# A two-layer graph network: the multiply by the adjacency matrix, split between VectorE and GpSimd two heads to two or one head to three

## The chip, the cores and the metric

One core of a Trainium2 chip runs the whole program. The metric is the device time in microseconds (us). A core has a matrix engine (TensorE, PE in the profile), a vector engine (VectorE, DVE), an activation engine (ScalarE, ACT), a general engine (GpSimd, POOL), a queue engine for transfers (SyncE, SP), an on-chip memory (SBUF) of 128 partitions, and an accumulator memory for TensorE's results (PSUM). Each engine runs its own instructions in order; engines wait for each other by semaphores.

## The reference

Two layers over the same 4096 x 4096 weighted adjacency matrix `adj`, with 4096 nodes of 512 features. Layer 0 is attention with `adj` added to its scores. Layer 1, where the change is, is a graph attention with 8 heads of 64 features:

```python
x = x + _L0_gnn_ref(h, adj, adj, Wq, bq, Wk, bk, Wv, bv)
h = jnp.maximum(_layernorm(x, axis=-1), 0.0)
...
nX = (x @ W).reshape(n, NHEAD, OUT_DIM).transpose(1, 0, 2)
nX = a_ln * (nX - mean) / (std + EPS) + b_ln
at1 = jnp.einsum('kno,ok->kn', nX, a1)[:, :, None]
at2 = jnp.einsum('kno,ok->kn', nX, a2)[:, :, None]
kg = at1 + at2.transpose(0, 2, 1)
kg = jax.nn.leaky_relu(kg, negative_slope=LK_ALPHA)
kg = kg * graph[None, :, :]
mg = jnp.where(mask[None, :, :], kg, NEG_FILL)
attention = jax.nn.softmax(mg, axis=-1)
y = attention @ nX + nX
return jax.nn.elu(y)
```

`graph` and `mask` are both `adj`. For each pair of nodes and each head the kernel must form a leaky logit, multiply it by the pair's weight, take the exponent and sum the features of the neighbours.

## The kernel before

**Layer 0** makes q, k and v, walks over 32 blocks of 128 rows, and on the way writes a transposed copy of `adj` to memory (`gT_d`, scaled by 0.2, and `nT_d`, a large negative number where a pair is not connected). Nothing of it is touched.

**Layer 1's start** (lines 316 to 453) projects the features, normalizes them per head into `nX`, and computes the two numbers per node and head that the logits are made of. It isn't touched either, but it runs GpSimd and VectorE instructions of width 512 whose lengths are of use: L405 and L399 on GpSimd, L396 and L397 on VectorE.

**Layer 1's loop** (lines 455 to 673) has 512 steps: 8 blocks of 512 target nodes (`ic`), 2 groups of 4 heads (`hg`), 32 blocks of 128 source nodes (`jt`). The 32 steps of one `(ic, hg)` are called a group in what follows; there are 16. The logits of a step lie transposed, source nodes on the partitions, in a tile `t` of 128 x 4 heads x 512 float32; five such tiles rotate. A step `n` consists of:

- `z_sums` (L513, L518): TensorE adds both numbers and the negative mask into PSUM, in two halves of two heads (tile `d`, three buffers).
- `relu` (L525): ScalarE makes the positive part for heads 0 and 1.
- `leaky` (L533 twice, L537): VectorE makes the logits, two heads by a maximum and an addition of PSUM (L533, 512 wide each), two by an addition of PSUM (L537, 1024 wide).
- `weigh` (L543 to L545): the multiply by the adjacency block `g`.
- `exponent` (L548): ScalarE takes the exponent of all four heads.
- `values` (L561): TensorE sums the features of the source nodes, eight matmuls.

The loop is software-pipelined by hand: iteration `n` issues `values(n-3)`, `exponent(n-2)`, `weigh(n-1)`, `leaky(n)`, `z_sums(n+1)`, `relu(n+1)`, in this order. Every engine follows this source order, since `seq` is `tc.keep_in_program_order`. So on VectorE the multiply of one step stands in front of the logits of the next one.

Three steps after a group's last one, `finish` starts its closing work, spread over the next iterations: a copy of the sums (L570 on ScalarE, L571 on VectorE); `rows_of` in the two iterations after, where TensorE turns the sums (L582) and VectorE divides them (L589 copy, L591 reciprocal, L592 a minimum over `low` and `tot`, L594 twice, all this for two halves); then `own` twice (L602, a GpSimd addition of width 512); `exps` on ScalarE (L609 to L611); `close` twice (L615 on VectorE, L619 on GpSimd, both of width 512), and a store. These stand after `leaky` and before the next `weigh` in each engine's order.

`weigh` before, with `gate` a tile of one column that nothing else reads:

```python
g = loads[n // JB][0][:, STEPS[n][2] % JB, :].unsqueeze(1).to_broadcast([P, 2, GC])
t = logits[n]
seq(nc.vector.tensor_mul(t[:, 0:2, :], t[:, 0:2, :], g))
seq(nc.gpsimd.tensor_mul(gate, t[:, 0, 0:1], t[:, 0, 0:1]))
seq(nc.gpsimd.tensor_mul(t[:, 2:4, :], t[:, 2:4, :], g))
```

The gate instruction (L544) reads a column that VectorE's multiply (L543) writes. GpSimd, which runs in order, therefore starts its own multiply (L545) only after VectorE's. The blocks of `g` come by transfers of four steps at a time (L466), two rounds ahead, into three buffers.

Of the kernel before, what the change touches and what calls it, by code (L numbers as in the profile page):

```python
# [10 lines left out]
F32 = mybir.dt.float32  # L11
# [7 lines left out]
P = 128  # L19
# [16 lines left out]
GC = 512  # L36
# [9 lines left out]
@with_exitstack  # L46
def adj_preln_gnn_kernel(
    ctx: ExitStack,
    tc: tile.TileContext,
    x: bass.AP,  # L50
    adj: bass.AP,
    wqT: bass.AP,
    bq: bass.AP,
    wkT: bass.AP,
    bk: bass.AP,
    wvT: bass.AP,
    bv: bass.AP,
    w1: bass.AP,
    a1T: bass.AP,
    a2T: bass.AP,  # L60
    a_ln: bass.AP,
    b_ln: bass.AP,
    out: bass.AP,
):
    nc = tc.nc
    keep = ctx.enter_context(tc.tile_pool(name="keep", bufs=1))
    flag = keep.tile([1, 1], mybir.dt.int32, name="flag")
    fast_path(
        tc, flag, x, adj, wqT, bq, wkT, bk, wvT, bv, w1, a1T, a2T, a_ln, b_ln, out
    )  # L70

    low = nc.values_load(flag[0:1, 0:1])
    with tc.If(low > 0):
        general_path(tc, x, adj, wqT, bq, wkT, bk, wvT, bv, w1, a1T, a2T, a_ln, b_ln, out)
# [3 lines left out]
def fast_path(  # L78
# [18 lines left out]
    nc = tc.nc  # L97
# [51 lines left out]
    with tc.tile_pool(name="kv", bufs=1) as kv:  # L149
# [3 lines left out]
        with tc.tile_pool(name="proj_c", bufs=1) as pc, tc.tile_pool(  # L153
            name="proj", bufs=2
# [45 lines left out]
        with tc.tile_pool(name="attn", bufs=2) as work, tc.tile_pool(  # L200
            name="attn_ps", bufs=2, space=PSUM
# [95 lines left out]
    gat = ctx.enter_context(tc.tile_pool(name="gat", bufs=1))  # L297
# [10 lines left out]
    HB = HD + 1  # L308
    back = gat.tile([P, 2, HB], F32, name="back")
    fours = gat.tile([P, P], BF16, name="fours")  # L310
    gate = gat.tile([P, 1], F32, name="gate")

    with tc.tile_pool(name="gat_c", bufs=1) as pc, tc.tile_pool(name="gat_w", bufs=2) as work, tc.tile_pool(
        name="gat_ps", bufs=2, space=PSUM
# [140 lines left out]
    with tc.tile_pool(name="ga", bufs=2) as work, tc.tile_pool(name="ga_ps", bufs=2, space=PSUM) as psum:  # L455
        JB = 4
        seq = tc.keep_in_program_order
        STEPS = [(ic, hg, jt) for ic in range(NI) for hg in range(NH // HG) for jt in range(NB)]
        n_steps = len(STEPS)
        loads, logits, zs, groups = {}, {}, {}, {}  # L460
# [77 lines left out]

        def weigh(n):

            g = loads[n // JB][0][:, STEPS[n][2] % JB, :].unsqueeze(1).to_broadcast([P, 2, GC])
            t = logits[n]
            seq(nc.vector.tensor_mul(t[:, 0:2, :], t[:, 0:2, :], g))  # L543
            seq(nc.gpsimd.tensor_mul(gate, t[:, 0, 0:1], t[:, 0, 0:1]))  # L544
            seq(nc.gpsimd.tensor_mul(t[:, 2:4, :], t[:, 2:4, :], g))  # L545

        def exponent(n):
            seq(nc.scalar.activation(logits[n], logits[n], AF.Exp, bias=shift))  # L548
# [93 lines left out]
        for n in range(n_steps + 14):  # L642
            if n % JB == 0 and n // JB + 2 < n_steps // JB:
                load_adj(n // JB + 2)
            if n < n_steps and STEPS[n][2] == 12:
                load_rows(n)
            if 0 <= n - 3 < n_steps:
                values(n - 3)
                if n % JB == 2:
                    loads.pop((n - 3) // JB)  # L650
            if 0 <= n - 2 < n_steps:
                exponent(n - 2)
            if 0 <= n - 1 < n_steps:
                weigh(n - 1)
            if n < n_steps:
                leaky(n)
            if n + 1 < n_steps:
                if STEPS[n + 1][2] == 0:
                    open_group(n + 1)
                z_sums(n + 1)  # L660
                relu(n + 1)
            if 0 <= n - 3 < n_steps and STEPS[n - 3][2] == NB - 1:
                finish(n, *STEPS[n - 3][:2])
            for f in later.pop(n, []):
                f()
# [411 lines left out]
```

## Time and profile before

| What | Value |
|---|---|
| Median of 3 runs | 4892.43 us (4891.4 to 4892.91) |
| The profiled execution's own time | 4892.91 us |
| Its span in the profile | 4891.1 us |
| Busy share of the span: PE, DVE, ACT, POOL | 90%, 63%, 42%, 32% |
| First and last start of L545 (layer 1's loop) | 2751.3 and 4867.8 us |
| DVE busy in 3500 to 4000 us | 478.23 of 500 us |
| PE busy in 3500 to 4000 us | 438.97 of 500 us |
| ACT and POOL busy in 3500 to 4000 us | 366.72 and 335.11 us |

The span is the time from the first to the last instruction that the profiler saw; the execution's own time lies 1.8 us above it. The shares over the whole span mix layer 0, in which TensorE is busiest, with layer 1's loop; the lower rows show the loop alone. POOL's busy time includes time in which an instruction of it has started and stands. Lines are named as in the profile, L543 for line 543; after the change the same code has numbers that are one lower up to the multiply on VectorE, and two lower behind it.

### The profile page before, as it was taken

To read this page: it belongs to the slowest core of one execution; us is meant where nothing else is said; L and a number is where in the kernel's file an instruction comes from. 1 tells how busy PE (TensorE), PEld (TensorE's weight loads), DVE (VectorE), ACT (ScalarE), POOL (GpSimd) and SP (SyncE) were. 2 spreads that over 40 slices of the span, in tenths; PEclk is the share of its full clock that TensorE was granted. 3 is DMA by queue.
4 is the path that set the end of the run, shared out by engine and by line. 5 is a ranking of instruction groups with operands and counts; after the bars stand their busy time and mean duration, and the time that the engine had idled before them with its cause. 6 is when DMAs were issued, how large, how long until landed. Compare 5 with 4: busy or idle time off the path is not lost.

```text
span 4891.1 us, 46208 instructions
## 1 busy us (share of the span) xinstructions
PE 4392.4 (90%) x16036; PEld 1780.2 (36%) x16036; DVE 3067.9 (63%) x5059; ACT 2057.5 (42%) x1908; POOL 1544.6 (32%) x1222
## 2 busy tenths in 40 slices
PE   8999999999999999999745588888888888888887
PEld 3444444444444444444322122222222222222222
DVE  3215333333333333333377799999999999999998
ACT  1112222112121211211111477777777777777776
POOL 0000000000000000000133466666766666666666
PEclk9999999999999999999867799999999999999999
DMA  2115333333233333332211333333333333333332
GB/s 88 48 30 164 96 98 98 97 92 94 91 94 97 97 97 98 97 98 75 66 56 55 115 120 114 115 108 121 123 112 120 114 116 113 115 118 114 110 113 74
DMA packets 521508, 484.23 MB, mean 99 GB/s; under 512 B 168624, under 2 KB 424624, under 8 KB 517168
## 3 DMA queue, kind: packets, MB, share of 16 engines
q1 hardware_dynamic: 229632, 371.24, 23.3%
q10 hardware_dynamic: 291632, 109.95, 8.0%
q8 instruction: 128, 2.10, 0.2%
q14 instruction: 116, 0.95, 0.1%
HBM read 342.69 MB, written 138.41 MB: 98 GB/s over the span
## 4 chain that ended last, share of the span: by engine, by line
PE 54%; DVE 30%; issue 12%; POOL 3%; DMA 1%; ACT 1%; SPq 0%; ACTq 0%; POOLq 0%; DVEq 0%
PE acc L257 18%; PE ps L238 18%; DVE t L533 13%; DVE t L537 10%; PE acc L561 3%; PE pq L175 2%; PE pv L195 2%; PE pk L186 2%; PE pg L220 2%; DVE t L543 2%; PE d L518 2%; PE pt L265 2%; POOL prod L405 2%; POOL own L399 1%; PE d L513 1%
## 5 line engine op out<-in xcount | busy, mean ns | idle before, releaser
L545 POOL TENSOR_TENSOR t<-t,g 128x1024 f32<-128x1024 f32 x512 | 1213.8, 2371 | 1.7 <-issue 1.6
L561 PE MATMUL acc<-t,nX 128*64 128x512 f32 x4096 | 1016.0, 618 | 47.5 <-ACT ob L570 24.7
L548 ACT ACTIVATE t<-t,shift 128x2048 f32<-128x2048 f32 x512 | 1019.6, 1991 | 2.4 <-POOL t L545 2.4
L257 PE MATMUL acc<-v,pT 128*128 128x512 f32 x2048 | 924.2, 594 | 2.6 <-ACT pT L267 0.4
L238 PE MATMUL ps<-kT,qt 128*128 128x512 f32 x2048 | 887.6, 593 | 0.7 <-DVE m L241 0.7
L401 POOL MEMSET nX<- 128x8 f32 x32 | 3.6, 113 | 2576.0 <-DVE full L396 2576.0
L525 ACT ACTIVATE t<-d 128x1024 f32<-128x1024 f32 x512 | 524.7, 1025 | 560.3 <-PE d L518 560.3
L533 DVE SCALAR_TENSOR_TENSOR t<-u,at2m,d 128x512 f32<-128x512 f32 x1024 | 713.3, 735 | 21.2 <-PE d L518 21.2
L543 DVE TENSOR_TENSOR t<-t,g 128x1024 f32<-128x1024 f32 x512 | 684.6, 1337 | 15.1
L267 ACT COPY pT<-pt 128x512 f32<-128x512 f32 x256 | 146.8, 586 | 1284.1 <-PE pt L265 1249.7
L537 DVE TENSOR_TENSOR t<-t,d 128x1024 f32<-128x1024 f32 x512 | 618.3, 1208 | 1.7 <-ACT t L525 1.2
L513 PE MATMUL d<-z,z 6*128 6x512 bf16 x2048 | 375.1, 386 | 204.5 <-DVE t L533 192.5
L238 PEld LDWEIGHTS ps<-kT,qt 128*128 128x128 f32 x2048 | 386.0, 190 | 470.6 <-issue 461.2
L518 PE MATMUL d<-nb,ident_b 128*128 128x512 bf16 x2048 | 547.4, 391 | 0.0
L257 PEld LDWEIGHTS acc<-v,pT 128*128 128x128 f32 x2048 | 369.2, 190 | 378.5 <-issue 368.2
L222 DVE TENSOR_SCALAR ng<-pg 128x512 bf16<-128x512 f32 x256 | 176.7, 691 | 459.2 <-PE pg L220 405.3
L561 PEld LDWEIGHTS acc<-t,nX 128*64 128x64 f32 x4096 | 253.2, 139 | 568.7 <-issue 464.4
L241 DVE CUSTOM_DVE_ANT_0 s<-ps,s 128x512 f32<-128x512 f32 x256 | 174.0, 690 | 449.8 <-PE ps L238 449.6
L513 PEld LDWEIGHTS <-z 6*128 6x128 bf16 x2048 | 92.4, 91 | 748.8 <-issue 703.4
L544 POOL TENSOR_TENSOR gate<-t 128x1 f32<-128x1 f32 x512 | 99.4, 194 | 707.6 <-DVE t L543 659.2
L224 ACT ACTIVATE gs<-pg 128x512 f32<-128x512 f32 x256 | 153.6, 600 | 328.0 <-DVE ng L222 243.4
L225 DVE SCALAR_TENSOR_TENSOR gs<-ng,gs 128x512 f32<-128x512 bf16 x256 | 174.0, 690 | 160.7 <-ACT gs L224 160.5
(118 smaller groups left out, 2886.4 us busy)
## 6 DMA issues: line engine op xcount, KB each, us to landing
g<-gT_d SPq DMA_DIRECT2D x128, 1024.0 KB, 5.4
s<-in_adj_dram SPq DMA_DIRECT2D x32, 2048.0 KB, 8.3
gT_d<-gs ACTq DMA_DIRECT2D x256, 256.0 KB, 2.3
nb<-nT_d SPq DMA_DIRECT2D x128, 512.0 KB, 3.6
nT_d<-ng ACTq DMA_DIRECT2D x256, 128.0 KB, 2.0
z<-z_d SPq DMA_DIRECT2D x144, 128.0 KB, 2.1
xt<-in_x_dram SPq DMA_DIRECT2D x8, 1024.0 KB, 5.3
q_d<-qs SPq DMA_DIRECT2D x32, 256.0 KB, 3.1
```

The source lines that it names most:

```text
L222: nc.vector.tensor_scalar(ng, pt, 0.0, NEG_BIG, ALU.is_equal, ALU.mult)
L238: nc.tensor.matmul(ps, qt[:, k, :], kT[:, k, ts(c, 512)], start=k == 0, stop=k == KC - 1)
L257: nc.tensor.matmul(acc, pT[:, ts(t, P)], v[:, j, :], start=j == 0, stop=j == NB - 1)
L513: seq(nc.tensor.matmul(pair[hh // 2][:, hh % 2, :], z2[rows, ts(jt % JB, P)], groups[ic, hg]["z1"][rows, :], start=True, stop=False,))
L518: seq(nc.tensor.matmul(pair[hh // 2][:, hh % 2, :], ident_b, ng[:, jt % JB, :], start=False, stop=True))
L525: seq(nc.scalar.activation(t[:, 0:2, :], zs[n][0], AF.Relu, scale=4.0))
L533: seq(nc.vector.scalar_tensor_tensor(t[:, 2 + e, :], u4[:, e, :], at2m[:, jt, h : h + 1], pair[1][:, e, :], ALU.max, ALU.add,))
L537: seq(nc.vector.tensor_add(t[:, 0:2, :], t[:, 0:2, :], pair[0]))
L543: seq(nc.vector.tensor_mul(t[:, 0:2, :], t[:, 0:2, :], g))
L545: seq(nc.gpsimd.tensor_mul(t[:, 2:4, :], t[:, 2:4, :], g))
L548: seq(nc.scalar.activation(logits[n], logits[n], AF.Exp, bias=shift))
L561: seq(nc.tensor.matmul(grp["acc"][hf][ts(e, HD), :], nX[:, jt, hg * HG + 2 * hf + e, :], t[:, 2 * hf + e, :], start=jt == 0, stop=jt == NB ...
```

## The change

In `weigh` the multiply by `g` is cut differently. VectorE takes one head (512 elements per partition) in place of two, GpSimd three (1536) in place of two. The gate instruction and its tile go, so nothing orders the two multiplies of a step any more: both wait for what wrote their part of `t`, which on both is VectorE's L537 of the same step. The order on each engine, given by `seq`, stays, and so do the results.

```diff
-    gate = gat.tile([P, 1], F32, name="gate")
...
         def weigh(n):
 
-            g = loads[n // JB][0][:, STEPS[n][2] % JB, :].unsqueeze(1).to_broadcast([P, 2, GC])
+            g = loads[n // JB][0][:, STEPS[n][2] % JB, :]
             t = logits[n]
-            seq(nc.vector.tensor_mul(t[:, 0:2, :], t[:, 0:2, :], g))
-            seq(nc.gpsimd.tensor_mul(gate, t[:, 0, 0:1], t[:, 0, 0:1]))
-            seq(nc.gpsimd.tensor_mul(t[:, 2:4, :], t[:, 2:4, :], g))
+            seq(nc.vector.tensor_mul(t[:, 0, :], t[:, 0, :], g))
+            seq(nc.gpsimd.tensor_mul(t[:, 1:4, :], t[:, 1:4, :], g.unsqueeze(1).to_broadcast([P, 3, GC])))
```

## The prediction

> **What bounds the kernel now.** I read the page's table of costly groups first, then the timeline of layer 1's loop for each engine alone, then the stretches where VectorE and GpSimd overlap. The groups give the price of each instruction (engine, operation, shapes, count, busy us, mean ns, idle time before):
>
> ```profile
> L545 POOL TENSOR_TENSOR t<-t,g 128x1024 f32<-128x1024 f32 x512 | 1213.8, 2371 | 1.7 <-issue 1.6
> ...
> L533 DVE SCALAR_TENSOR_TENSOR t<-u,at2m,d 128x512 f32<-128x512 f32 x1024 | 713.3, 735 | 21.2 <-PE d L518 21.2
> L543 DVE TENSOR_TENSOR t<-t,g 128x1024 f32<-128x1024 f32 x512 | 684.6, 1337 | 15.1
> ```
>
> The loop runs 512 steps, and in most of them VectorE's timeline (start, length, both in us) is this:
>
> ```profile
> 3734.36 1.39 DVE L533 SCALAR_TENSOR_TENSOR t<-u,at2m,d 128x512 f32<-128x512 f32 x2
> 3735.68 1.21 DVE L537 TENSOR_TENSOR t<-t,d 128x1024 f32<-128x1024 f32 x1
> 3736.92 1.26 DVE L543 TENSOR_TENSOR t<-t,g 128x1024 f32<-128x1024 f32 x1
> 3738.10 1.39 DVE L533 SCALAR_TENSOR_TENSOR t<-u,at2m,d 128x512 f32<-128x512 f32 x2
> ```
>
> Each starts when the one before ends, and the step is 3738.10 - 3734.36 = 3.74 us. So VectorE is the bound. GpSimd is not:
>
> ```profile
> 3734.58 0.19 POOL L544 TENSOR_TENSOR gate<-t 128x1 f32<-128x1 f32 x1 [1.22 <-DVE t L543]
> 3734.72 2.38 POOL L545 TENSOR_TENSOR t<-t,g 128x1024 f32<-128x1024 f32 x1
> ```
>
> It idles 1.22 us a step until L543 is done, since the gate instruction L544 reads what L543 wrote. The two multiplies by g therefore never run side by side in this step. TensorE is close behind: in the stretch 3734.36 to 3738.10 it is busy 3.54 of 3.74 us. ScalarE has 2.91.
>
> Where a stray GpSimd instruction breaks that order, the trace shows what running side by side costs:
>
> ```profile
> 3697.01 2.37 POOL L545 TENSOR_TENSOR t<-t,g 128x1024 f32<-128x1024 f32 x1
> ...
> 3698.25 2.21 DVE L543 TENSOR_TENSOR t<-t,g 128x1024 f32<-128x1024 f32 x1
> ...
> 3699.34 2.26 POOL L602 TENSOR_TENSOR y<-y,own 128x512 f32<-128x512 f32 x1
> ...
> 3701.55 0.19 POOL L544 TENSOR_TENSOR gate<-t 128x1 f32<-128x1 f32 x1
> ```
>
> L543 needs 1.21 us alone and took 2.21: it stood until L545 was through, and then ran. L602 needs 1.26 us alone (the last two have that) and took 2.26: it stood until L543 was through. They alternate and do not share, and VectorE, waiting since 3698.25, went ahead of the GpSimd instruction queued behind L545. This is so in every group of the loop. Even a tiny operand is caught, in the tail:
>
> ```profile
> 4877.90 1.26 POOL L602 TENSOR_TENSOR y<-y,own 128x512 f32<-128x512 f32 x1 [7.74 <-DVE tot L589]
> 4877.92 0.18 DVE L591 RECIPROCAL rinv<-tot 128x4 f32<-128x4 f32 x1
> 4878.02 1.16 DVE L592 TENSOR_TENSOR low<-low,tot 128x4 f32<-128x4 f32 x1
> ```
>
> L592 is usually 0.13 us; here it stood about 1.03 us for L602. L533 and L537 keep their lengths beside L545.
>
> **What the Trainium skill says.** "SBUF — State Buffer", section "Who interferes with whom": a VectorE instruction with two SBUF inputs contends with a GpSimd instruction that reads SBUF, the one that starts second blocks fully; one with at most one SBUF input does not contend. The trace agrees on both: L543 and L592 have two SBUF inputs, L533 and L537 take their pair from PSUM. The page doesn't say who goes first when both wait; the trace above does. "GPSIMD Engine Reference", section 3.1, has GpSimd 1.96 times slower at a two-input operation; here 2.371 against 1.21 us, the same ratio.
>
> **The change, part by part.**
> (1) VectorE's multiply shrinks from 1024 to 512 elements. The same shape in the projection (L396) takes 0.67 us, so VectorE's own work per step falls by 0.53 us to about 3.2.
> (2) GpSimd's grows to 1536. 128x512 takes 1.265 (L405) and 128x1024 2.371, so 1.106 per further 512: 3.477 us. Instructions queued back to back overlap by about 0.04, so 3.44 from start to start.
> (3) The gate goes: 512 times 0.19 us of GpSimd, which lay in idle time, and with it the order. GpSimd now waits for L537 of its step, as VectorE's multiply does. VectorE starts it at once; GpSimd comes second, and stands.
> (4) What VectorE's multiply adds to GpSimd's cycle. In the stretch above, L602 and the 1024-wide L543 together took 3701.55 - 3699.34 = 2.21 from GpSimd's start to its next start; L602 alone is 1.265 - 0.04. The insertion costs 0.985 for 1024 elements, less 0.535 for the 512 that go: 0.45 us. Ends: 0.67 if nothing of it overlaps; as low as 0.3 if more does.
>
> The steady step: 3.44 + 0.45 = 3.89 us, against 3.745 (the usual distance of L545's starts): +0.15. VectorE has its 2.5 us of L533 and L537 done before GpSimd releases, so its next multiply always waits there first and the alternation is stable. ScalarE's exponent waits for GpSimd later by a microsecond in each step, with several tiles t in hand (five buffers), and TensorE has 0.35 us a step to spare: both stay hidden. The loads of g are two rounds ahead and stay so.
>
> (5) The ends of the 15 groups before the last; there seven steps are unusual. I call L537's end zero.
> - The two steps with the row sums (L589 to L594) last 7.6 us each on average. VectorE there waits 1.9 us for TensorE's L582 (1.3 in the second), and GpSimd stands behind the gate. Without the gate it runs in this hole, and L592 runs into it. First step: GpSimd is still at the step before until +0.75, then at this step's multiply until +4.2; L592, due at +2.2, stands until then; 1.32 us of the rest, 0.62 of multiply and 2.52 of L533 and L537 follow: 8.6 us. Second: GpSimd runs from +0.1 to +3.5, L592 stands from +1.55, and its second copy at +4.3 meets L602, which has just started (as in the tail): about 1.03 more, 9.0 in all. So +1.0 and +1.4.
> - The two steps with L602 take 4.68 each now. The first L602 has gone into the step before: 3.9, so -0.8. The second: 3.44 + 0.45 + 1.22 = 5.1, so +0.4.
> - The two with L615 and L619 take 5.3 now. L615 has two SBUF inputs and stands for GpSimd; then its 0.65, the multiply 0.55, L619 1.15 and 3.4 of GpSimd follow one another: 5.8, so +0.5 twice.
> - The step with L571's copy has 4.18 now and hides it: -0.3.
> Sum per group +2.7 us. From below it is 0, where TensorE's delays cover the lock; from above 5.
>
> Sum: 512 - 15 x 7 = 407 steps x 0.15 = 61, and 15 x 2.7 = 40: +101 us. The tail changes by well under 1. The profiled execution has span 4891.1, ran 4892.91, and the median is 4892.43. 4891.1 + 101 is 4992 for the span and 4994 for the median. Nothing is left to hide it: no other engine waits long enough elsewhere.
>
> **The rivals.**
> A, faster. VectorE's short multiply slips past GpSimd's long one for less than 0.30 us, the 3.745 - 3.44 from which this decides. With none at all, TensorE's 3.54 becomes the bound: 407 x 0.2 = 83, and some 1.5 us at each group's end, 22: about 4787. For it: VectorE is the bound and loses 0.53 us a step. Against it: 1024 elements cost 0.985, and even 4 elements stood 1.03 us.
> B, much slower. When GpSimd releases, its own queued multiply goes first, and VectorE waits for two. Then two steps take 0.55 + 3.44 + 3.44 + 0.55 + 2.6 = 10.6 us, 5.3 each: 407 x 1.55 = 631, with the ends about 5565. For it: both wait at that moment. Against it: L543 won that meeting in each group's end.
> C, no change: the step comes out between 3.73 and 3.76, and the ends even out: 4892. It asks for an insertion of 0.3 exactly.
> That the change doesn't do what it says is out: GpSimd's instruction stream shows one 128x1536 multiply a step, no gate, waiting for VectorE's addition.
>
> **The numbers.** Forecast 0.85, A 0.06, B 0.06, C 0.03. The forecast's own ends: with 3.40 for the 1536 multiply and no cost at the groups' ends the step is 3.81 and the sum +27, 4920; with 0.67 of insertion and 5 us at the ends it is 407 x 0.37 + 75 = 226, 5118. Few of these ends meet, so I take 4935 to 5085. A change of 0.2% (10 us) is what a measurement of this kernel can tell from none. Faster 0.06, same 0.03, slower 0.91.
>
> **What would show it.** Right: L545's successor near 3.45 to 3.5 us with GpSimd busy nearly without a gap in the steady steps; VectorE's multiply stretched from 0.67 to about 1.3 by its wait; step 3.89; L592 at up to 2 us, 30 or more times. Wrong: if VectorE's multiply stays at 0.67 beside GpSimd's (A), or if it lasts 4 us in every second step (B). If GpSimd's 1536 elements take more than 3.6 us, (2) is mis-sized.

## The result and the profile after

The median is 4962.89 us (4961.42 to 4965.52, 4 runs) against 4891.91 before in the same comparison; the ratio is 1.0147, with a 95% interval of 1.0129 to 1.0164. The change makes the kernel 71 us slower. The span of the profiled execution went from 4891.1 to 4959.5, +68.4 us.

Some groups of the page after the change (L543 is now GpSimd's multiply, L542 VectorE's, L532 and L536 what were L533 and L537):

```profile
L543 POOL TENSOR_TENSOR t<-t,g 128x1536 f32<-128x1536 f32 x512 | 1950.4, 3843 | 147.7 <-DVE t L536 76.4
...
L532 DVE SCALAR_TENSOR_TENSOR t<-u,at2m,d 128x512 f32<-128x512 f32 x1024 | 713.4, 735 | 26.9 <-DMA g<-gT_d 16.3
...
L542 DVE TENSOR_TENSOR t<-t,g 128x512 f32<-128x512 f32 x512 | 668.6, 1306 | 15.1
```

VectorE's multiply has half the elements and still 1306 ns on average (1337 before): the saving has gone into standing. L532 keeps its 735 ns. GpSimd has 147.7 us of idle time left before its multiplies. Before the change it idled 707.6 us before its gates, most of it for VectorE's multiply:

```profile
L544 POOL TENSOR_TENSOR gate<-t 128x1 f32<-128x1 f32 x512 | 99.4, 194 | 707.6 <-DVE t L543 659.2
```

VectorE's timeline in the steady part, and GpSimd's row from the same stretch (three multiplies merged into one row of 11.65 us):

```profile
3658.63 1.40 DVE L542 TENSOR_TENSOR t<-t,g 128x512 f32<-128x512 f32 x1
3659.43 11.65 POOL L543 TENSOR_TENSOR t<-t,g 128x1536 f32<-128x1536 f32 x3
3659.95 1.39 DVE L532 SCALAR_TENSOR_TENSOR t<-u,at2m,d 128x512 f32<-128x512 f32 x2
3661.26 1.21 DVE L536 TENSOR_TENSOR t<-t,d 128x1024 f32<-128x1024 f32 x1
3662.50 1.38 DVE L542 TENSOR_TENSOR t<-t,g 128x512 f32<-128x512 f32 x1
```

The step is 3662.50 - 3658.63 = 3.87 us. VectorE looks as full as before, but of L542's 1.39 us about 0.7 is waiting (it takes 0.67 alone). A row's length is the time from start to end, with the standing in it: a busy engine need not be the one that works.

The two steps with the row sums in one group, first VectorE's timeline, then GpSimd's, same stretch:

```profile
3712.05 1.31 DVE L590 TENSOR_TENSOR low<-low,tot 128x4 f32<-128x4 f32 x1
...
3719.15 2.06 DVE L590 TENSOR_TENSOR low<-low,tot 128x4 f32<-128x4 f32 x1
...
3721.81 1.16 DVE L590 TENSOR_TENSOR low<-low,tot 128x4 f32<-128x4 f32 x1
```

```profile
3709.87 3.47 POOL L543 TENSOR_TENSOR t<-t,g 128x1536 f32<-128x1536 f32 x1
3717.74 3.46 POOL L543 TENSOR_TENSOR t<-t,g 128x1536 f32<-128x1536 f32 x1 [4.40 <-issue]
3721.69 1.26 POOL L600 TENSOR_TENSOR y<-y,own 128x512 f32<-128x512 f32 x1 [0.50 <-DVE tot L587]
```

Four elements per partition take up to 2.06 us. Each of the three ends within 0.1 us of GpSimd's instruction (3713.34, 3721.20, 3722.95): L590 stands for it. Of all 64, 33 took over 1 us. Their minimum, median and maximum (in ns) follow; before, the median was 131:

```profile
L590 DVE TENSOR_TENSOR low<-low,tot x64: 129/1124/2069, 2885.6 to 4946.4; 128x4 f32<-128x4 f32 x64
```

Where the 68.4 us lie, from the starts of L537 (L536 after) in all 512 steps, as means over the 15 groups after the first:

| Steps of a group | Before, us | After, us | Difference |
|---|---|---|---|
| two with the row sums | 7.59 + 7.57 | 8.61 + 8.81 | +2.26 |
| the one after them | 3.75 | 3.39 | -0.36 |
| two with GpSimd's first additions | 4.75 + 4.62 | 4.22 + 4.53 | -0.61 |
| the one with L571's copy | 4.18 | 3.87 | -0.31 |
| three with the last additions | 14.32 | 15.21 | +0.89 |
| the other 23 | 86.5 | 89.1 | +2.6 |

That is +4.5 a group. The 15 groups give 67 us and the first group 2.8; the loop began 2.6 earlier, and what follows its last step took 0.8 longer.

### The profile page after: what moved, and what is told of

The parts are those of the page before. It is cut to its first block, busy times and chain, and to the rows that moved or that the text cites. A ratio compares the mean times of both kernels' runs of the same rounds, so it can differ in the third digit from the quotient of the medians.

```text
span 4959.5 us, 44909 instructions
## 1 busy us (share of the span) xinstructions
PE 4410.4 (89%) x16036; PEld 1779.5 (36%) x16036; DVE 3118.6 (63%) x5059; ACT 2059.9 (42%) x1908; POOL 2168.7 (44%) x710
## 4 chain that ended last, share of the span: by engine, by line
PE 47%; DVE 26%; issue 12%; POOL 4%; ACT 2%; DMA 1%; ACTq 0%; SPq 0%; DVEq 0%; POOLq 0%
PE acc L257 18%; PE ps L238 17%; DVE t L532 11%; DVE t L536 9%; PE acc L559 3%; PE d L517 3%; PE pg L220 2%; PE pt L265 2%; POOL t L543 2%; POOL prod L404 2%; DVE t L542 1%; DVE low L590 1%; PE d L512 1%; POOL own L398 1%; PE pt L580 1%
## 5 line engine op out<-in xcount | busy, mean ns | idle before, releaser
L543 POOL TENSOR_TENSOR t<-t,g 128x1536 f32<-128x1536 f32 x512 | 1950.4, 3843 | 147.7 <-DVE t L536 76.4
L559 PE MATMUL acc<-t,nX 128*64 128x512 f32 x4096 | 1046.8, 634 | 56.9 <-ACT t L546 32.2
L532 DVE SCALAR_TENSOR_TENSOR t<-u,at2m,d 128x512 f32<-128x512 f32 x1024 | 713.4, 735 | 26.9 <-DMA g<-gT_d 16.3
L542 DVE TENSOR_TENSOR t<-t,g 128x512 f32<-128x512 f32 x512 | 668.6, 1306 | 15.1
L536 DVE TENSOR_TENSOR t<-t,d 128x1024 f32<-128x1024 f32 x512 | 618.5, 1208 | 6.9 <-ACT t L524 5.3
L512 PE MATMUL d<-z,z 6*128 6x512 bf16 x2048 | 357.9, 388 | 245.3 <-DVE t L532 196.9
L517 PEld LDWEIGHTS <-ident_b 128*128 128x128 bf16 x2048 | 161.0, 99 | 249.0 <-issue 133.4
```

The source lines that it names most:

```text
L512: seq(nc.tensor.matmul(pair[hh // 2][:, hh % 2, :], z2[rows, ts(jt % JB, P)], groups[ic, hg]["z1"][rows, :], start=True, stop=False,))
L517: seq(nc.tensor.matmul(pair[hh // 2][:, hh % 2, :], ident_b, ng[:, jt % JB, :], start=False, stop=True))
L532: seq(nc.vector.scalar_tensor_tensor(t[:, 2 + e, :], u4[:, e, :], at2m[:, jt, h : h + 1], pair[1][:, e, :], ALU.max, ALU.add,))
L536: seq(nc.vector.tensor_add(t[:, 0:2, :], t[:, 0:2, :], pair[0]))
L542: seq(nc.vector.tensor_mul(t[:, 0, :], t[:, 0, :], g))
L543: seq(nc.gpsimd.tensor_mul(t[:, 1:4, :], t[:, 1:4, :], g.unsqueeze(1).to_broadcast([P, 3, GC])))
```

## The experiments

Two theories stood for the steady step. L: the two multiplies exclude each other, and VectorE's is inserted into each cycle of GpSimd's. G: GpSimd's 1536 elements simply take that long.

**No multiply on VectorE.** One head of each four is left unweighted.

```diff
-            seq(nc.vector.tensor_mul(t[:, 0, :], t[:, 0, :], g))
             seq(nc.gpsimd.tensor_mul(t[:, 1:4, :], t[:, 1:4, :], g.unsqueeze(1).to_broadcast([P, 3, GC])))
```

> The changed kernel without VectorE's multiply: head 0 of each group of four isn't multiplied by g, the rest is as after the change. Theory L (the two multiplies exclude each other, and VectorE's adds 0.42 us to each cycle of GpSimd's): the steady step falls from 3.87 to what is next, GpSimd's 3.44 or TensorE's 3.54, and the time from 4963 to about 4800 to 4820. Theory G (no exclusion, GpSimd's 1536 elements simply need 3.87 us): the step stays at 3.87 and the time within 20 us of 4950.

Measured: 4738.36 us, ratio 0.9681 (0.9665 to 0.9697). The steady step is 3.42 to 3.43 us, with GpSimd busy without a gap. GpSimd's group:

```profile
L542 POOL TENSOR_TENSOR t<-t,g 128x1536 f32<-128x1536 f32 x512 | 1754.9, 3472 | 131.5 <-issue 57.0 <-DVE t L536 46.1 <-DMA xi<-x_d 25.3
```

The same instruction that has a mean of 3843 ns beside VectorE's multiply has 3472 without it. G is out. The insertion of 512 elements costs 3.87 - 3.425 = 0.445 us. The time came out 62 us below the lower end of what L had expected, since I had taken TensorE's busy 3.54 us as a floor; TensorE kept up with 3.42. In a stretch of the first group (2766.3 to 2782.1 us), while GpSimd, at 3.43 us a multiply, was falling behind, the steps even took 3.16 us, with TensorE busy 15.75 of 15.80 us.

**The new split, with the gate kept.**

```diff
-            seq(nc.vector.tensor_mul(t[:, 0:2, :], t[:, 0:2, :], g))
+            seq(nc.vector.tensor_mul(t[:, 0, :], t[:, 0, :], g))
             seq(nc.gpsimd.tensor_mul(gate, t[:, 0, 0:1], t[:, 0, 0:1]))
-            seq(nc.gpsimd.tensor_mul(t[:, 2:4, :], t[:, 2:4, :], g))
+            seq(nc.gpsimd.tensor_mul(t[:, 1:4, :], t[:, 1:4, :], g.unsqueeze(1).to_broadcast([P, 3, GC])))
```

> The kernel before with the new split, one head to three, but with the gate kept. Theory L: GpSimd's release, then VectorE's multiply 0.55, the semaphore and the gate 0.29, then 3.43 of GpSimd, one after the other: a steady step of 4.27 and a time of about 5105; L592 stays at 0.13 us and the two steps with the row sums go back to about 7 us. Theory G: VectorE's multiply has long been done when GpSimd comes to the gate, which adds 0.15 only: 4.0 us a step, 4990.

Measured: 5127.97 us, ratio 1.0478 (1.046 to 1.0495); the steady step is 4.29, the row-sum steps 7.09 and 7.0 on average. Both engines, from VectorE's timeline and from GpSimd's:

```profile
3826.66 1.21 DVE L537 TENSOR_TENSOR t<-t,d 128x1024 f32<-128x1024 f32 x1
3827.91 2.75 DVE L543 TENSOR_TENSOR t<-t,g 128x512 f32<-128x512 f32 x1
```

```profile
3826.52 0.19 POOL L544 TENSOR_TENSOR gate<-t 128x1 f32<-128x1 f32 x1
3826.66 3.44 POOL L545 TENSOR_TENSOR t<-t,g 128x1536 f32<-128x1536 f32 x1
```

VectorE's multiply waits until 3830.10, when the GpSimd one of the step before ends, and is through at 3830.66. With the gate the three waits follow one another, as L had it. So three heads on GpSimd cost far more with the gate than without it. What the gate's removal costs at this split is at the groups' ends, where the two row-sum steps take 8.61 and 8.81 us without it.

**The old split, without the gate.**

```diff
             seq(nc.vector.tensor_mul(t[:, 0:2, :], t[:, 0:2, :], g))
-            seq(nc.gpsimd.tensor_mul(gate, t[:, 0, 0:1], t[:, 0, 0:1]))
             seq(nc.gpsimd.tensor_mul(t[:, 2:4, :], t[:, 2:4, :], g))
```

> The kernel before with its split of two heads to two, only the gate taken away. Theory L: in a steady step VectorE's multiply starts first on its own, GpSimd stands 1.1 us for it and is done 0.3 us before the next one, so the step stays at 3.745; at the groups' ends L592 runs into GpSimd's multiply and into L602, some +0.5 to +1.5 us a group: 4895 to 4915. If the gate's removal as such were what cost 70 us, this run would show it: about 4960.

Measured: 5406.47 us, ratio 1.1049 (1.103 to 1.1067), a steady step of 4.92. Neither number had been expected. VectorE's timeline and GpSimd's:

```profile
3709.07 1.39 DVE L532 SCALAR_TENSOR_TENSOR t<-u,at2m,d 128x512 f32<-128x512 f32 x2
3710.39 1.21 DVE L536 TENSOR_TENSOR t<-t,d 128x1024 f32<-128x1024 f32 x1
3711.63 2.44 DVE L542 TENSOR_TENSOR t<-t,g 128x1024 f32<-128x1024 f32 x1
```

```profile
3710.64 2.35 POOL L543 TENSOR_TENSOR t<-t,g 128x1024 f32<-128x1024 f32 x1 [2.57 <-DVE t L532]
```

GpSimd's part here is heads 2 and 3, which L532 writes. So it is released by L532, at 3710.64, and not by L536, which ends at 3711.60. It is first, and VectorE's multiply stands 1.2 us in every step, on the engine that is the bound. My expectation had GpSimd second because both wait for L536; that holds for the change under study, where GpSimd also takes head 1, and not here. TensorE's granted clock was lower in this run (0.84 in 3705 to 3725 us), but VectorE was busy 19.86 of these 20 us and waited for nothing from TensorE, so the clock doesn't explain the step. This made a theory of its own, F: what decides is whose multiply starts first.

**The old share of work, cut by columns, without the gate.** It tests F: with a column cut GpSimd needs all four heads, and so L536.

```diff
-            seq(nc.vector.tensor_mul(t[:, 0, :], t[:, 0, :], g))
-            seq(nc.gpsimd.tensor_mul(t[:, 1:4, :], t[:, 1:4, :], g.unsqueeze(1).to_broadcast([P, 3, GC])))
+            CUT = 256
+            seq(nc.vector.tensor_mul(
+                t[:, :, 0:CUT], t[:, :, 0:CUT], g[:, 0:CUT].unsqueeze(1).to_broadcast([P, HG, CUT])
+            ))
+            seq(nc.gpsimd.tensor_mul(
+                t[:, :, CUT:GC], t[:, :, CUT:GC], g[:, CUT:GC].unsqueeze(1).to_broadcast([P, HG, GC - CUT])
+            ))
```

> No gate and half the work to each engine, as in the run that took 5406 us, but cut by columns: VectorE takes columns 0 to 255 of all four heads, GpSimd 256 to 511 of all four. Both now wait for VectorE's addition (L537 of the kernel before). Theory F (what decides is who gets to g first: there GpSimd waited only for the two maxima and was 1 us ahead of VectorE's multiply, here VectorE is first): the steady step is 3.75 again, with 0.5 to 1.5 us more at a group's end, 4895 to 4915. Theory G2 (two heads' worth on each without a gate always collide): 4.9 a step, 5400.

Measured: 4898.92 us, ratio 1.0013 (1.0006 to 1.002), a steady step of 3.71. VectorE's timeline and GpSimd's:

```profile
3871.14 1.23 DVE L543 TENSOR_TENSOR t<-t,g 128x1024 f32<-128x1024 f32 x1
3872.28 1.40 DVE L532 SCALAR_TENSOR_TENSOR t<-u,at2m,d 128x512 f32<-128x512 f32 x2
```

```profile
3871.18 3.42 POOL L546 TENSOR_TENSOR t<-t,g 128x1024 f32<-128x1024 f32 x1 [0.29 <-DVE t L536]
```

The same numbers of elements as in the run of 5406 us. VectorE is first by 0.04 us, and GpSimd stands for about 1.05 of its 3.42 us, where nobody waits for it. Cutting by columns does not by itself change a multiply's length: the shortest take 1.209 us on VectorE and 2.342 on GpSimd here, 1.206 and 2.345 in the kernel before. F holds: 508 us lie between the two runs, and the difference is what GpSimd's operand depends on. Against the kernel before, which has the gate, this run gains nothing.

**The minimum from PSUM**, on the changed kernel, for the groups' ends. The rival (E) was that TensorE's L580 (L582 of the kernel before) is late there.

```diff
-                    seq(nc.vector.tensor_tensor(low[:, ts(k, 4)], low[:, ts(k, 4)], tot, ALU.min))
+                    seq(nc.vector.tensor_tensor(low[:, ts(k, 4)], low[:, ts(k, 4)], v[:, :, HD], ALU.min))
```

> The changed kernel with one operand of the minimum (L590 there) read from PSUM in place of the copy in SBUF, so that it has one SBUF input; same result. Theory L: it no longer stands for GpSimd: about 0.15 us in all 64 places, the two row-sum steps fall from 8.6 and 8.8 to about 7.4 and 6.7 (a little more where TensorE is late), half a microsecond is given back in the step with GpSimd's first addition: 25 to 45 us less than 4963, the steady step stays at 3.87. Theory E (the row-sum steps are long since TensorE's L580 comes late): no change, 4963 within 8.

Measured: 4942.79 us, 20 us below the changed kernel's median, which was measured beside other runs of the kernel before; the ratios are 1.0101 (1.0085 to 1.0118) and 1.0147 (1.0129 to 1.0164), which don't overlap. The minimum no longer stands anywhere:

```profile
L590 DVE TENSOR_TENSOR low<-low,pt x64: 126/128/130, 2887.4 to 4927.5; 128x4 f32<-128x4 f32 x64
```

The gain is less than the 25 us expected at the least, and the row-sum steps fall to 8.2 and 7.9 us on average, less far than expected. The first has two kinds of lengths, 7.3 to 7.5 us in 4 of the 15 groups and 8.3 to 8.6 in 11. Around a long one the stretches read (us, then busy us and count of PE, PEld, DVE, ACT and POOL, the granted clock, the DMA share, GB/s):

```profile
3145.00:3153.00 8.00, 6.53 (x31) 1.84 (x32) 7.96 (x10) 6.48 (x5) 8.00 (x3) 1.00 0.48 147
3153.00:3158.00 5.00, 4.27 (x14) 1.00 (x15) 2.66 (x4) 2.58 (x3) 5.00 (x2) 0.66 0.33 107
3158.00:3164.00 6.00, 4.48 (x26) 2.06 (x25) 4.39 (x14) 2.92 (x2) 1.92 (x1) 1.00 0.17 30
```

TensorE's clock is 0.66 there, against 1.00 in the stretches around it, and a set of eight matmuls takes 3.58 us in place of 1.94. All 11 long groups have such a slow set (3.3 to 3.6 us), and none of the 4 short ones. So L and E are both right in part. In the changed kernel 5 groups have a slow set, and in 4 of them the step is only up to 0.1 us longer than in the others: there the lock hid it. Why it comes in 11 groups once L590 no longer stands is open.

**A version that beats both.** By the sums found here the load can be balanced: VectorE's chain is 2.6 us and about 1.04 us per 1000 elements of its multiply, GpSimd's cycle its own multiply and the insertion. Two cuts by columns, with the minimum from PSUM:

> The same cut at column 224 (VectorE 896 elements, GpSimd 1152), and the minimum reads PSUM. By the lock: VectorE's chain is 2.6 + 0.94 = 3.55 us, GpSimd's cycle 0.85 + 2.61 = 3.46, so VectorE sets 3.55 to 3.6 a step, and the time is 4765 to 4820, below both kernels. If GpSimd's exclusive time is what any version without a gate pays, it isn't below 4890.

Measured: 4835.0 us, ratio 0.9884 (0.9867 to 0.99), a steady step of 3.57.

> The cut at column 216 (864 and 1184 elements), where both sums meet: VectorE 3.51, GpSimd 0.81 + 2.69 = 3.50. 0 to 20 us below the cut at 224 if the sums hold; above it if the two chains get in each other's way when they are equal.

Measured: 4811.91 us, ratio 0.9837 (0.982 to 0.9853), a steady step of 3.54. The steps are as expected to 0.03 us. The first time is 15 us above the range given for it, and the second 23 us below the first, where 0 to 20 had been expected. One step of each group takes 6.1 us in both. VectorE's timeline of the cut at 216 there, and GpSimd's (two multiplies in one row, the second from 3897.57 on):

```profile
3896.26 1.22 DVE L536 TENSOR_TENSOR t<-t,d 128x1024 f32<-128x1024 f32 x1
3897.39 0.69 DVE L574 COPY ob<-acc 128x512 f32<-128x512 f32 x1
3897.99 3.18 DVE L543 TENSOR_TENSOR t<-t,g 128x864 f32<-128x864 f32 x1
```

```profile
3894.03 6.23 POOL L546 TENSOR_TENSOR t<-t,g 128x1184 f32<-128x1184 f32 x2
```

The copy of the sums (L571 of the kernel before) stands between the addition and the multiply. GpSimd, released by the addition, goes first, and the multiply stands over 2 us, until 3900.26: F again. The last run takes the copy away from VectorE:

```diff
-            seq(nc.vector.tensor_copy(ob[:, 1, :], grp["acc"][1]))
+            seq(nc.scalar.copy(ob[:, 1, :], grp["acc"][1]))
```

> The cut at column 216 with the copy of the second half of a group's sums (L571 of the kernel before) on ScalarE in place of VectorE. Theory F (who gets to g first): in the cut kernels that copy stands between VectorE's addition and its multiply, GpSimd, released by the addition, is first there, and VectorE's multiply stands over 2 us, so that this one step of each group takes 6.15 us; without the copy it falls to 3.6 to 4.2, and the time by 25 to 40 us from 4812, less what TensorE waits longer for the sums (0.6 us a group, 9 us). Rival (the step is long since TensorE, slowed in its clock, is late there): no change, 4812 within 8.

Measured: 4788.21 us, ratio 0.9792 (0.9776 to 0.9808). The step fell from 6.15 to 3.54, and the first row-sum step behind it rose from 6.5 to 7.8: 39 us gained in 15 groups, half of it given back. The longer step is a wait for TensorE: its L585 (L582 of the kernel before), which turns the sums, starts 2.7 us after VectorE's addition in 14 of the 15 groups, where it started 1.3 to 1.8 us after it with the copy on VectorE.

## Why the prediction was right, point by point

- **The lock sets the step.** Forecast 3.44 + 0.45 = 3.89 us; measured 3.87, of which 3.425 is GpSimd alone and 0.445 the insertion. The run without VectorE's multiply shows both terms by themselves.
- **A sign that was set wrongly.** GpSimd's multiply was to show 3.45 to 3.5 us, and more than 3.6 us was to mean that its 1536 elements had been priced too low. It shows 3.843 on average. Yet the price was right (3.425 alone); the row also holds the time for which it stands for VectorE's multiply, 0.45 us a step in the forecast itself.
- **VectorE goes first when both wait.** In the steady steps L542 waits first and is let in each time (the step stays within some hundredths of 3.87 us); nothing like the 5.3 us of rival B appears.
- **The gain per step.** 61 us had been summed for 407 ordinary steps; those steps gave 39. About 10 is 0.125 us in place of 0.15. The step after the row sums has the largest miss of any one step: I had it at 3.89, but GpSimd has caught up by then, so that VectorE's own 3.2 shows in most groups. It is 3.39 on average, 0.5 below, 8 us in all. Most of the remaining 4 us lies in the third step of a group, which fell from 3.74 to 3.60 where it had been set to rise.
- **The groups' ends.** 40 us forecast, 31 measured. Row sums: +1.0 and +1.4 forecast, +1.02 and +1.24 measured; the minimum took over 1 us in 33 places, where 30 or more had been forecast. The copy: -0.3, as forecast. The first additions: -0.4 forecast, -0.6 measured, but in parts -0.8 and +0.4 against -0.5 and -0.1, so the sum is nearer than its parts. The last two: +1.0 forecast, +0.75 measured; the forecast took both for 5.3 us before, but the second had 4.67.
- **Rival A's bound was wrong.** TensorE's busy 3.54 us was taken as its floor. The run without VectorE's multiply went at 3.42, and at 3.16 in places. It did not touch the forecast.
- **GpSimd comes second, for a reason that holds for this split only.** Both multiplies wait for L537 here, as the prediction said. With the old split they would not; that run's 5406 us shows how much hung on it.
- **Two readings of the kernel before that were not quite right.** L533 and L537 take one of their two inputs from PSUM, not both. And the two multiplies do meet in the steady step: L543 starts at 3736.92, 0.18 us before L545 ends at 3737.10. It takes 1.26 us there and 1.23 in the steady steps of the cut at 256, where it is first, and the steps are 3.74 and 3.71. So VectorE was the bound, but by an estimate from these two runs the lock cost about 0.03 us a step already.

So the direction and the mechanism held, and the sum (+101 against +68 in the span) was too large mostly by the ordinary steps (61 against 39) and, less, by the ends. The misses of the ends partly cancel, which is luck.

## What to carry to other kernels

Where instructions of two engines exclude each other, as the two multiplies do here, count them as users of one resource: add up what each adds to the cycle, and ask which engine arrives first. Give the first place to the engine that is the bound. At two heads' worth on each, an extra waiting instruction did that (4892 us), and so did a cut in which both multiplies depend on the same addition (4899); with neither it took 5406. Then look at the small instructions with both inputs in SBUF in the rare steps, since each can stand for what is left of the other engine's instruction: here 4 elements per partition took up to 2.07 us.

## What the runs showed of the hardware

- An inserted VectorE multiply costs GpSimd's cycle less than its own length: 0.445 us for 512 elements that take 0.67 alone (3.87 us a step against 3.425).
- The rows of an engine that stands count as busy: GpSimd's multiply of 1536 elements shows 3.43 to 3.99 us for the same work, and VectorE's minimum of 4 elements 0.13 to 2.07.
- A minimum with one input in PSUM took 0.13 us in all 64 places beside GpSimd, where the one with both in SBUF had a median of 1.12.
- TensorE was busy 3.54 us in a step of 3.74, and ran the same step in 3.42 and in 3.16 us.
- In some groups' ends TensorE's granted clock fell to 0.66, and eight matmuls took 3.58 us in place of 1.94.
